# POOL's side steps and the x add of a four-block kernel, each held behind what is written before it on its engine

## The chip, the cores and the metric

The kernel runs on one core of one Trainium2 chip. The metric is device time in microseconds (us) of one execution. Before the change three executions took 3738.57, 3738.6 and 3734.69 us; the median is 3738.57 us.

## What is computed

`x` has shape (4, 1024, 128). Four blocks follow one another, each of the form

```
xn = layernorm(x)
s  = attention-like branch of block i on xn
g  = silu(feed-forward-like branch of block i on xn)
x  = x + s * g
```

- Block 0: windowed attention with rotary positions, 16 heads of 8; the other branch is a channel mix.
- Block 1: causal attention; the other branch is a mixture of 8 experts, of which each token uses 2.
- Block 2: full attention followed by a feed-forward network of its own (`_ffn`: residual sum, layernorm, 128 to 512 to 128, residual sum). The other branch is a switch layer: each token goes to one of 8 experts, at most 80 tokens to each.
- Block 3: a state-space (Mamba) block; the other branch is two layers of local attention with gated feed-forward.

The switch layer of block 2 in the reference, shortened:

```python
probs = softmax(tokens @ gate_w + gate_b)
expert_idx = argmax(probs)
pos = position of the token in its expert's queue
keep = pos < 80
dispatch = tokens placed by (expert, pos)          # scatter
h = gelu(dispatch @ w1 + b1)
expert_out = h @ w2 + b2
out = expert_out gathered by (expert, pos) * gate_prob   # 0 where not kept
```

## The kernel before

The rows are held as 32 tiles of 128 tokens by 128 channels, 8 tiles for each of 4 batches. `xn` and `s` stay in on-chip memory for all batches. `x` itself is parked in device memory between blocks. The program is written as Python lists of small steps. `_interleave` mixes several lists into one written order: the longest list sets the number of turns, and in each turn every list, in the order given, is advanced to the same share of its length.

A planner then decides the order of issue on each engine. It goes by its own estimates of when each instruction's inputs are there and takes what is ready, so an instruction may be issued ahead of ones that are written before it on its engine. `keep_in_program_order` adds an edge from an instruction to the one written just before it on the same engine: issue order only, with no wait for the other to finish. All matmuls and transposes of TensorE already have it (`_mm`, `_tr`, L78 and L82). Nothing on the other engines has it before the change. Each engine works its queue in order, so an instruction that waits also holds what is queued behind it.

Attention of blocks 0 to 2 (`_attention`) goes in 16 units, n = 4b + g for batch b and group g of 4 heads. In unit n the following are interleaved, in this order:

- `ahead`: the row maxima of the next units (PE products into `max_ps`, L78; DVE reduction into `neg`, L344), then the split of `neg` into three bf16 parts on POOL (L163 to L166) and its spreading into rows of q (PE, DVE L368, DMA L371). The split for unit n+1 stands in unit n, near 60% of it.
- `weights`: scores on PE (`sc`), exponentials on ACT (L417), products with the values on PE. In units 4, 8 and 12, the first of a batch, the end of the batch before is put in as well: `finish(b)` writes its part of `s` (L504 or L506).
- for g = 0 to 2, a part of `project(b+1)`: both halves of q and the first half of k for g = 0; the second half of k and the stores for g = 1; the values for g = 2. In block 2 a half of q or k is moved out of PSUM by ACT (L232, L235), multiplied with the rotary tables on POOL (L236 to L238) and after the second half split into three parts, also on POOL (L163 to L166).
- the side steps that a plan assigns to the unit.

The plan of block 2 (`_blocks12`, units 0 to 15) is:

| units | side steps |
|---|---|
| 0 to 2 | update of block 1 for batch 3, and the switch's logits |
| 3 | routing: `rows`, the place of every token |
| 4 to 8 | `sends`: 32 scatters of a tile of `xn` into `sent`, indirect DMAs issued by POOL (L1039); 6, 6, 7, 6 and 7 of them |
| 5 to 7, 9 to 11, 13 to 15 | `_ffn` of batch 0, 1, 2: POOL sum `s += xn` (L789), layernorms (DVE L60, L61, L63, L69 and POOL L65), POOL bias sum (L793), then hidden and output products, DVE sum (L787) |
| 9 to 11 | the experts: load of `sent` (SP, L1051), products, store into `back` (L1077) |
| 12, 13, 15 | `gates(b)` of batch 0, 1, 2: 8 gathers from `back` into `xn`, indirect DMAs issued by POOL (L1083), a pause, the weighing on POOL (L1086), Silu on ACT (L653) |
| 13, 14 | `_end_steps` of batch 0 and 1: the update (below) and a copy on POOL (L1781) |

After unit 15 come `_ffn` of batch 3 beside `_end_steps(2)` and `gates(3)`, and last `_end_steps(3)`. The update (`_update_steps`, used at the end of blocks 0, 1 and 2 for every batch, twelve times in all) fetches x, multiplies `xn = s * xn` on POOL (L151), adds `x += xn` on DVE (L148), stores x (L149, SP queue) and normalizes for the next block.

Full attention has 32 maxima steps per unit, 12 of which are done a unit early; with the split and the spreading that makes 34 steps of `ahead`, and with the end of the batch before 38 steps of `weights` in units 4, 8 and 12. In block 2 POOL has nothing else to do in a unit than the split, the rope where there is a projection, and the side steps. In blocks 0 and 1 it also masks the weights (L387).

Of the kernel before, what the change touches and what calls it, by code (L numbers as in the profile page):

```python
# [25 lines left out]
ALU = mybir.AluOpType  # L26
# [3 lines left out]
P = 128  # L30
B, T, C = 4, 1024, 128
NT = T // P
# [21 lines left out]
def _layernorm_parts(k, src, dst):  # L54

    nc, n = k.nc, src.shape[1]
    st = k.small.tile([P, n, 6], F32, tag="ln_st", name="ln_st")
    mv = k.small.tile([P, n, 2], F32, tag="ln_mv", name="ln_mv")
    for i in range(n):
        nc.vector.bn_stats(out=st[:, i, :], in_=src[:, i, :])  # L60
        nc.vector.bn_aggr(out=mv[:, i, :], in_=st[:, i, :])  # L61
    ve = k.small.tile([P, n], F32, tag="ln_ve", name="ln_ve")
    nc.vector.tensor_scalar_add(ve, mv[:, :, 1], EPS)  # L63
    rs = k.small.tile([P, n], F32, tag="ln_rs", name="ln_rs")
    nc.gpsimd.tensor_tensor(rs, ve, k.neghalf[:, :n], ALU.pow)  # L65

    def apply():
        for i in range(n):
            nc.vector.tensor_scalar(  # L69
                dst[:, i, :], src[:, i, :], mv[:, i, 0:1], rs[:, i : i + 1], ALU.subtract, ALU.mult  # L70
            )

    return apply


def _mm(k, *args, **kw):

    k.tc.keep_in_program_order(k.nc.tensor.matmul(*args, **kw))  # L78
# [3 lines left out]
    k.tc.keep_in_program_order(k.nc.tensor.transpose(*args))  # L82


def _ps1(k, name, shape=(P, 512), dtype=F32):

    return k.ps.tile(list(shape), dtype, tag="s", name=name, bufs=3)


def _ps2(k, name):  # L90

    return k.ps.tile([P, 2, 512], F32, tag="m", name=name, bufs=2)


def _to_fm(k, src, dst, scale=None, bias=None):

    nc, n = k.nc, src.shape[1]
    ps = _ps1(k, "tr_ps", (P, 4, P))
    for i in range(n):
        _tr(k, ps[:, i, :], src[:, i, :], k.ident)  # L100
    flat = ps[:, :n, :].rearrange("p a b -> p (a b)")
    if scale is None:
        nc.scalar.copy(dst, flat)
    else:
        nc.vector.tensor_scalar(dst, flat, scale, bias, ALU.mult, ALU.add)


def _norm_steps(k, src, dst):

    held = {}  # L110

    def part(i):
        a = slice(4 * i, 4 * i + 4)
        return [
            lambda: held.update({i: _layernorm_parts(k, src()[:, a, :], dst[:, a, :])}),
            lambda: held.pop(i)(),
        ]

    (a0, b0), (a1, b1) = part(0), part(1)
    return [a0, a1, b0, b1]  # L120
# [10 lines left out]
def _x_tile(k, of):  # L131
    x = k.xpool.tile([P, NT, C], F32, tag="x", name="x", bufs=2)
    k.nc.sync.dma_start(x, of)
    return x


def _update_steps(k, b, of):

    nc = k.nc
    a = slice(b * NT, b * NT + NT)  # L140
    s, g = k.s[:, a, :], k.xn[:, a, :]
    held = {}

    def fetch():
        held["x"] = _x_tile(k, of)

    def add():
        nc.vector.tensor_tensor(held["x"], held["x"], g, ALU.add)  # L148
        nc.sync.dma_start(k.parked[b], held["x"])  # L149

    steps = [fetch, lambda: nc.gpsimd.tensor_tensor(g, s, g, ALU.mult), None, add]  # L151
    return steps + _norm_steps(k, lambda: held["x"], g)


# [495 lines left out]
def _silu_steps(k, batches):  # L650
    g = k.xn
    return [
        lambda a=slice(b * NT, b * NT + NT): k.nc.scalar.activation(g[:, a, :], g[:, a, :], AF.Silu)  # L653
        for b in batches
    ]
# [85 lines left out]
def _ffn(k, pool, w, b):  # L741


    nc, s, xT = k.nc, k.s, k.xT
    a = slice(b * NT, b * NT + NT)
    held = {}

    def norm(i):
        c = slice(b * NT + 4 * i, b * NT + 4 * i + 4)
        held["x", i] = xn = pool.tile([P, 512], F32, tag="side", name="ln_x", bufs=2).rearrange(  # L750
            "p (n c) -> p n c", c=C
        )
        held["n", i] = _layernorm_parts(k, s[:, c, :], xn)

    def to_fm(i):
        _to_fm(k, held.pop(("x", i)), xT[:, b, 1 + 512 * i : 513 + 512 * i], w["g2"], w["be2"])

    def hidden(n, f2):
        hp = _ps2(k, "hp2")
        held["h", n, f2] = h = pool.tile([P, 2, 512], F32, tag="pt", name="h2", bufs=5)  # L760
        for ff in range(2):
            f = 2 * f2 + ff
            rhs = xT[:, b, 1 + 512 * n : 513 + 512 * n]
            _mm(k, hp[:, ff, :], lhsT=w["f1"][:, f * P : f * P + P], rhs=rhs, start=True, stop=True)
            nc.scalar.activation(h[:, ff, :], hp[:, ff, :], AF.Relu, bias=w["fb1"][:, f : f + 1])

    def output(n, f2):
        h = held.pop(("h", n, f2))
        if f2 == 0:
            held["op", n] = _ps1(k, "op2", (P, 4, P))  # L770
        op = held["op", n]


        for c in range(4):
            for ff in range(2):
                _mm(
                    k,
                    op[:, c, :],
                    lhsT=h[:, ff, c * P : c * P + P],
                    rhs=w["f2"][:, 2 * f2 + ff, :],  # L780
                    start=f2 == 0 and ff == 0 and c == 0,
                    stop=f2 == 1 and ff == 1,
                    skip_group_check=True,
                )
        if f2 == 1:
            to = s[:, b * NT + 4 * n : b * NT + 4 * n + 4, :]
            nc.vector.tensor_tensor(to, to, held.pop(("op", n)), ALU.add)  # L787

    steps = [lambda: nc.gpsimd.tensor_tensor(s[:, a, :], s[:, a, :], k.xn[:, a, :], ALU.add), None]  # L789
    for i in range(2):  # L790
        steps += [lambda i=i: norm(i), None, lambda i=i: held.pop(("n", i))(), lambda i=i: to_fm(i)]
    bias = w["fb2"].unsqueeze(1).to_broadcast([P, NT, P])
    steps.append(lambda: nc.gpsimd.tensor_tensor(s[:, a, :], s[:, a, :], bias, ALU.add))  # L793
    for n in range(2):
        steps += [lambda n=n: hidden(n, 0), lambda n=n: hidden(n, 1)]
        steps += [lambda n=n: output(n, 0), lambda n=n: output(n, 1)]
    return steps
# [79 lines left out]
def _blocks12(k, t, wp, pool_of, gates, last, weights):  # L877
# [58 lines left out]
    with pool_of("a2") as pool:  # L936
        rope = pool.tile([P, 2, T], F32, name="rope")
        nc.sync.dma_start(rope, t["rope"][:, 1])
        begin, rest = _attention(k, pool, "full", xT, wb, s, rope)
        _interleave(moe(pool, B - 1), begin)  # L940
        route, experts, gates = _switch(k, pool, wp, t, lg2)

        plan = {}
        _put(plan, to_block2(B - 1, pool), range(3))
        _put(plan, route, [3])
        for b in range(B - 1):
            _put(plan, _ffn(k, pool, wb, b), _behind(b))
        sends, layers = experts
        _put(plan, sends, range(4, 9))
        _put(plan, layers, range(9, 12))  # L950
        for b in range(B - 1):
            _put(plan, gates(b), [12 + b + b // 2])
            if b < 2:
                _put(plan, _end_steps(k, b), [13 + b])
        rest(plan)
        steps = _ffn(k, pool, wb, B - 1)
        _run(steps[:2])
        _interleave(steps[2:], _end_steps(k, B - 2) + gates(B - 1))
        _run(_end_steps(k, B - 1))


def _switch(k, pool, wp, t, lg):
# [7 lines left out]
    nc, xn = k.nc, k.xn  # L970
# [3 lines left out]
    prob = pool.tile([P, NTILE], F32, name="prob")  # L974
    sent = k.tc.dram_tile([NS + P, C], F32, name="sent")
    back = k.tc.dram_tile([NS + P, C], F32, name="back")
# [12 lines left out]
    held = {}  # L989
# [30 lines left out]
    def place():  # L1020
# [12 lines left out]
        nc.vector.tensor_tensor(base, base, place, ALU.mult)  # L1033
        nc.vector.tensor_scalar(rows, base, own[:, 1:2], None, ALU.add)

    row_of = lambda n: bass.IndirectOffsetOnAxis(ap=rows[:, n : n + 1], axis=0)

    def send(n):
        nc.gpsimd.indirect_dma_start(out=sent, out_offset=row_of(n), in_=xn[:, n, :], in_offset=None)  # L1039

    def fetch(e):
        w1, w2 = (wp.tile([P, 512], F32, tag="ew", name="ew", bufs=3) for _ in range(2))
# [36 lines left out]
    def gates(b):  # L1079
        a = slice(b * NT, b * NT + NT)  # L1080

        def fetch(n):
            nc.gpsimd.indirect_dma_start(out=xn[:, n, :], out_offset=None, in_=back, in_offset=row_of(n))  # L1083

        def weigh():
            nc.gpsimd.tensor_tensor(  # L1086
                xn[:, a, :], xn[:, a, :], prob[:, a].unsqueeze(2).to_broadcast([P, NT, C]), ALU.mult
            )

        return [lambda n=n: fetch(n) for n in range(b * NT, b * NT + NT)] + [None, weigh] + _silu_steps(k, [b])  # L1090

    sends = [lambda n=n: send(n) for n in range(NTILE)]
    experts = [load, None, turn, lambda: fetch(0)]
    for e in range(E8):
# [940 lines left out]
```

## Time and profile before

| what | value |
|---|---|
| median of three executions | 3738.57 us |
| the profiled execution | 3753.32 us |
| its span, first to last instruction | 3751.6 us |
| mean granted PE clock | 0.915 |
| PE busy | 3242.6 us, 86% |
| DVE busy | 2440.5 us, 65% |
| ACT busy | 1985.6 us, 53% |
| POOL busy | 1440.0 us, 38% |
| sends L1039 | 32, first at 1793.8, last at 1892.5 us |
| gathers L1083 | 32, first at 2368.7, last at 2655.7 us |
| sums L789 | 4, first at 1887.4, last at 2643.1 us, 2.34 us each |
| products L151 | 12, 2.35 us each |
| adds L148 | 12, 1.23 us each in the median |

The page gives busy times by engine, the span in slices, the DMA queues and the costliest groups of instructions. A query of the trace gives for a stretch of time the busy time of each engine, the instructions of one engine in order (start, duration, engine, line, operation, output and input, and in brackets how long the engine had been idle and what released it), and who waited for whom. A wait for several things is put down to the one that came last.

### The profile page before, as it was taken

To read this page: it belongs to the slowest core of one execution; us is meant where nothing else is said; L and a number is where in the kernel's file an instruction comes from. 1 tells how busy PE (TensorE), PEld (TensorE's weight loads), DVE (VectorE), ACT (ScalarE), POOL (GpSimd) and SP (SyncE) were. 2 spreads that over 40 slices of the span, in tenths; PEclk is the share of its full clock that TensorE was granted. 3 is DMA by queue.
4 is the path that set the end of the run, shared out by engine and by line. 5 is a ranking of instruction groups with operands and counts; after the bars stand their busy time and mean duration, and the time that the engine had idled before them with its cause. 6 is when DMAs were issued, how large, how long until landed. Compare 5 with 4: busy or idle time off the path is not lost. (4 is left out here: it accounts for less than half of the span.)

```text
span 3751.6 us, 64824 instructions
## 1 busy us (share of the span) xinstructions
PE 3242.6 (86%) x24729; PEld 1738.2 (46%) x24729; DVE 2440.5 (65%) x4924; ACT 1985.6 (53%) x4189; POOL 1440.0 (38%) x1972
## 2 busy tenths in 40 slices
PE   5889999999898895899679998678589999989897
PEld 3545555654343432533223333222256667666665
DVE  6666654457757751788567675572478888877785
ACT  2444453346545552266456576456266666766674
POOL 5564554012313224030330210310476677656663
PEclk8998898999979987999889999789789999999999
DMA  3222212112212102111111021110211001011110
GB/s 95 68 68 48 60 39 85 39 32 48 55 29 65 38 14 59 33 36 26 33 39 26 22 60 36 41 26 1 71 25 21 18 20 27 20 24 23 27 24 22
DMA packets 132806, 144.96 MB, mean 39 GB/s; under 512 B 80264, under 2 KB 107792, under 8 KB 125328
## 3 DMA queue, kind: packets, MB, share of 16 engines
q1 hardware_dynamic: 130448, 136.62, 15.0%
q0 software_dynamic: 2048, 4.20, 0.4%
q8 instruction: 196, 3.21, 0.3%
q14 instruction: 114, 0.93, 0.1%
HBM read 92.72 MB, written 30.08 MB: 33 GB/s over the span
## 5 line engine op out<-in xcount | busy, mean ns | idle before, releaser
L417 ACT ACTIVATE pt<-sc 128x512 f32<-128x512 f32 (+3 forms) x2432 | 1077.0, 512 | 872.3 <-PE sc L78 845.7
L344 DVE TENSOR_REDUCE neg<-max_ps 128x1 f32<-128x1024 f32 (+6 forms) x1088 | 1178.4, 1102 | 503.6 <-PE max_ps L78 490.0
L78 PE MATMUL max_ps<-k,q 72*128 72x512 bf16 (+3 forms) x2304 | 673.0, 362 | 140.2 <-DVE neg L344 93.8
L78 PE MATMUL sc<-q,k 75*128 75x512 bf16 (+3 forms) x2432 | 680.3, 354 | 108.0 <-ACT pt L417 84.5
L78 PE MATMUL o_ps<-pt,va 128*32 128x512 f32 (+3 forms) x4864 | 584.8, 550 | 3.1 <-POOL pt L387 2.8
L387 POOL TENSOR_SCALAR_AFFINE_SELECT pt<-pt 128x256 f32<-128x256 f32 (+2 forms) x768 | 292.4, 398 | 615.3 <-ACT pt L417 612.9
L78 PEld LDWEIGHTS <-k 75*128 75x128 bf16 x2432 | 188.2, 101 | 538.3 <-issue 446.3
L78 PEld LDWEIGHTS <-q 72*128 72x128 bf16 x2304 | 227.8, 101 | 435.9 <-issue 313.7
L163 POOL CAST negp<-neg 128x32 bf16<-128x32 f32 x48 | 10.0, 209 | 806.2 <-DVE neg L344 805.9
L1593 ACT ACTIVATE pr<-lsc,nb,r 128x128 f32<-128x128 f32 x512 | 202.1, 475 | 61.5 <-DVE nb L1585 57.9
L1514 POOL TENSOR_TENSOR qn<-qn,rot 128x512 f32<-128x512 f32 x128 | 165.7, 1300 | 143.5 <-DVE rot L1506 127.8
L1523 POOL TENSOR_TENSOR rn<-ss,neghalf 128x16 f32<-128x16 f32 x64 | 188.7, 2949 | 66.7 <-DVE ss L1521 56.9
L78 PEld LDWEIGHTS <-ident 128*128 128x128 bf16 x1472 | 151.6, 103 | 106.0 <-issue 42.7
L78 PEld LDWEIGHTS o_ps<-pt,va 128*32 128x32 f32 x4864 | 101.2, 111 | 206.7 <-issue 167.7
L691 ACT ACTIVATE h<-hp,eb 128x512 f32<-128x512 f32 x128 | 80.8, 683 | 204.7 <-PE hp L78 197.1
L78 PE MATMUL hp<-xT,ew 128*128 128x512 f32 x256 | 132.8, 644 | 28.7 <-ACT rope_t L235 16.4
L1431 PE MATMUL qk_ps<-wqkv,hT 128*128 128x512 f32 x256 | 136.7, 618 | 24.1 <-DVE hT L1477 10.3
L78 PE MATMUL max_ps<-mask_window,ident 128*128 128x134 bf16 (+2 forms) x960 | 139.1, 228 | 0.0
L78 PEld LDWEIGHTS op<-ew,h 128*128 128x128 f32 x1024 | 125.8, 195 | 20.1 <-issue 17.7
L701 DVE SCALAR_TENSOR_TENSOR xn<-op,gates,xn 128x128 f32<-128x128 f32 x256 | 72.1, 345 | 94.3 <-PE op L78 94.3
L78 PE MATMUL op<-ew,h 128*128 128x128 f32 x1024 | 127.7, 279 | 0.0
L1582 DVE TENSOR_REDUCE top<-lsc 128x4 f32<-128x512 f32 x128 | 82.6, 683 | 43.7 <-PE lsc L1431 43.5
(346 smaller groups left out, 5492.1 us busy)
## 6 DMA issues: line engine op xcount, KB each, us to landing
q<-qx SPq DMA_DIRECT2D x144, 192.0 KB
k<-kx SPq DMA_DIRECT2D x432, 64.0 KB
va<-vb SPq DMA_DIRECT2D x120, 128.0 KB
x<-x SPq DMA_DIRECT2D x20, 512.0 KB
qx<-qp SPq DMA_DIRECT2D x12, 768.0 KB
kx<-kp SPq DMA_DIRECT2D x12, 768.0 KB
ew<-in_e1w_dram SPq DMA_DIRECT2D x64, 128.0 KB
x<-in_x_dram SPq DMA_DIRECT2D x8, 512.0 KB
```

Of the source, the lines that this page charges most:

```text
L78: k.tc.keep_in_program_order(k.nc.tensor.matmul(*args, **kw))
L163: eng.tensor_copy(dst[:, 0], src)
L344: nc.vector.tensor_reduce(neg[:, j0 : j0 + m, qt0], of, AX.X, ALU.max, negate=True)
L387: nc.gpsimd.affine_select(out=pt, in_=pt, pattern=[[0, 2], [step, pt.shape[2]]], compare_op=ALU.is_ge, fill=0.0, base=base, channel_multip ...
L417: nc.scalar.activation(pt[:, j % 2, :width], sc[:, :width], AF.Exp, scale=scale)
L691: nc.scalar.activation(h[:, hh, :], hp[:, hh, :], AF.Gelu, bias=eb1[:, e, hh : hh + 1])
L701: nc.vector.scalar_tensor_tensor(to, op[:, c, :], gates[:, 4 * n + c, e : e + 1], to, ALU.mult, ALU.add)
L1431: pin(nc.tensor.matmul(*args, **kw))
L1514: nc.gpsimd.tensor_tensor(qn[:, i], qn[:, i], rot, ALU.add)
L1523: nc.gpsimd.tensor_tensor(rn, ss.rearrange("p w h -> p (w h)"), k.neghalf[:, : 2 * NH], ALU.pow)
L1582: nc.vector.tensor_reduce(top, t.sc[r], AX.X, ALU.max)
L1593: nc.scalar.activation(t.pr[:, h, :], t.sc[r][:, c, :], AF.Exp, bias=t.nb[r][:, c : c + 1], scale=t.r8[:, h : h + 1])
```

## The change

The POOL sums and products of the update, of `_ffn` and of the weighing, both kinds of indirect DMA, and the update's add on DVE are passed through `keep_in_program_order`. What they compute and where they are written stays as it was. `_update_steps` is shared, so its product and its add are held in blocks 0 and 1 as well. The rotary products, the splits, the layernorms, the copy L1781 and everything on ACT and SP are left to the planner.

```diff
+def _tt(k, engine, *args):
+
+    k.tc.keep_in_program_order(engine.tensor_tensor(*args))
...
     def add():
-        nc.vector.tensor_tensor(held["x"], held["x"], g, ALU.add)
+        _tt(k, nc.vector, held["x"], held["x"], g, ALU.add)
         nc.sync.dma_start(k.parked[b], held["x"])
 
-    steps = [fetch, lambda: nc.gpsimd.tensor_tensor(g, s, g, ALU.mult), None, add]
+    steps = [fetch, lambda: _tt(k, nc.gpsimd, g, s, g, ALU.mult), None, add]
...
-    steps = [lambda: nc.gpsimd.tensor_tensor(s[:, a, :], s[:, a, :], k.xn[:, a, :], ALU.add), None]
+    steps = [lambda: _tt(k, nc.gpsimd, s[:, a, :], s[:, a, :], k.xn[:, a, :], ALU.add), None]
...
-    steps.append(lambda: nc.gpsimd.tensor_tensor(s[:, a, :], s[:, a, :], bias, ALU.add))
+    steps.append(lambda: _tt(k, nc.gpsimd, s[:, a, :], s[:, a, :], bias, ALU.add))
...
+    pin = k.tc.keep_in_program_order
     row_of = lambda n: bass.IndirectOffsetOnAxis(ap=rows[:, n : n + 1], axis=0)
 
     def send(n):
-        nc.gpsimd.indirect_dma_start(out=sent, out_offset=row_of(n), in_=xn[:, n, :], in_offset=None)
+        pin(nc.gpsimd.indirect_dma_start(out=sent, out_offset=row_of(n), in_=xn[:, n, :], in_offset=None))
...
         def fetch(n):
-            nc.gpsimd.indirect_dma_start(out=xn[:, n, :], out_offset=None, in_=back, in_offset=row_of(n))
+            pin(nc.gpsimd.indirect_dma_start(out=xn[:, n, :], out_offset=None, in_=back, in_offset=row_of(n)))
 
         def weigh():
-            nc.gpsimd.tensor_tensor(
-                xn[:, a, :], xn[:, a, :], prob[:, a].unsqueeze(2).to_broadcast([P, NT, C]), ALU.mult
-            )
+            _tt(k, nc.gpsimd, xn[:, a, :], xn[:, a, :], prob[:, a].unsqueeze(2).to_broadcast([P, NT, C]), ALU.mult)
```

## The prediction

> **What bounds the kernel now.** I first read the busy shares: PE (TensorE) is busy 86% of the span, DVE 65%, ACT 53%, POOL 38%. PE is the bound, so time is won only where PE stands still. Block 2 runs from about 1440 to 2690 us; its table of 20 us stretches has two places where PE nearly stops (columns: stretch, length, then busy us and count of PE, PEld, DVE, ACT, POOL, PE clock, DMA).
>
> ```profile
> 1820.00:1840.00 20.00, 19.19 (x112) 8.10 (x110) 16.06 (x16) 11.72 (x22) 6.70 (x7) 1.00 0.12 34
> 1840.00:1860.00 20.00, 2.01 (x14) 0.60 (x7) 0.00 (x0) 2.24 (x5) 10.49 (x10) 0.61 0.07 23
> 1860.00:1880.00 20.00, 0.00 (x0) 0.00 (x0) 0.00 (x0) 0.00 (x0) 10.63 (x11) 0.50 0.07 23
> 1880.00:1900.00 20.00, 7.51 (x30) 1.62 (x30) 7.42 (x27) 3.73 (x8) 14.38 (x14) 0.61 0.25 83
> ...
> 2380.00:2400.00 20.00, 0.58 (x1) 0.11 (x1) 3.48 (x2) 6.40 (x8) 15.08 (x11) 0.50 0.25 70
> ...
> 2440.00:2460.00 20.00, 3.75 (x12) 0.54 (x12) 13.67 (x55) 5.69 (x7) 11.66 (x13) 0.54 0.09 28
> ```
>
> In hole A (1842 to 1892) only POOL works. Next the waits in 1835 to 1900, engine by engine (total us, times, longest):
>
> ```profile
> PE max_ps L78 <- DVE neg L344: 49.7, 1, 49.7
> DVE ln_st L60 <- POOL s L789: 51.2, 1, 51.2
> POOL sent L1039 <- DMA sent<-xn,rows: 23.1, 15, 1.6
> ```
>
> So PE waits for row maxima, DVE cannot take them because a layernorm of `_ffn` (L60) stands ahead of them in its queue, and that waits for the sum `s += xn` (L789) on POOL. POOL's timeline says why the sum is late:
>
> ```profile
> 1853.86 0.96 POOL L1039 DMA_INDIRECT sent<-xn,rows  x1 [1.53 <-DMA sent<-xn,rows]
> 1854.84 1.27 POOL L236 TENSOR_TENSOR qd<-qd,rope 128x512 f32<-128x512 f32 x1
> ...
> 1887.45 2.34 POOL L789 TENSOR_TENSOR s<-s,xn 128x1024 f32<-128x1024 f32 x1
> ```
>
> Thirty of the 32 sends run ahead of L789, each 2.49 us after the last. They are written over units 4 to 8 but were issued as soon as `rows` existed. Holes B and C (2372 to 2403, 2438 to 2457), waits in 2335 to 2470:
>
> ```profile
> PE sc L78 <- ACT pt L417: 35.1, 6, 25.4
> PE max_ps L78 <- DVE neg L344: 12.4, 2, 10.1
> ACT L653 <- DMA xn<-back,rows: 17.9, 2, 13.4
> DVE x L148 <- POOL xn L151: 24.3, 2, 21.9
> ```
>
> ```profile
> 2391.68 2.36 POOL L151 TENSOR_TENSOR xn<-s,xn 128x1024 f32<-128x1024 f32 x1
> ...
> 2438.26 0.94 POOL L1083 DMA_INDIRECT xn<-back,rows  x1 [0.31 <-issue]
> 2440.90 1.90 POOL L1086 TENSOR_TENSOR xn<-xn,prob 128x1024 f32<-128x1024 f32 x1 [1.70 <-DMA xn<-back,rows]
> 2442.74 0.21 POOL L163 CAST negp<-neg 128x32 bf16<-128x32 f32 x1
> ```
>
> ACT waits in a Silu, DVE in an `x` add, both for gathers (L1083) of batches 0 and 1 that went together early in unit 12; then batch 2's gathers, written in unit 15, go ahead of the split for unit 13.
>
> [...] 2.2 us to landing, 2.49 us from send to send, with the rope products behind. [...] Two max_ps matmuls take 1.01 us after hole A and 0.60 before it; after B it stays slow for 19 us[...]. [...]
>
> **The change part by part.** Nothing is added or removed: 88 POOL instructions (32 sends, 32 gathers, 12 products L151, 4 sums L789, 4 L793, 4 weighings L1086) and 12 DVE adds L148 get an order edge to the instruction written before them on their engine.
>
> (1) Sends. Six stay in unit 4: one behind the rope of q's first half, the others spread. The unit runs from split to split, 1789.51 to 1894.54, 105.0 us; unit 8, with the same projection steps, 2068.91 to 2134.16, 65.3. Gain by that twin 39.8. By the hole: 49.7 idle plus 3.5 for slow clock (8.6 us after it, 1891.7 to 1896.3 and 1902 to 1906, at 1.01 for 0.60), less 5.6 because DVE waits that long for L789 before unit 9 and may now do so in unit 5: 47.6. I take **43**, between the two. A send that waits 1.5 us for the one before holds the rope and the splits queued behind it, and through them ACT's projections and the neg rows. At 6 or 7 sends in a unit of 50 to 65 us they stand some 8 us apart and POOL is idle more than half of the time (6.1 busy of 20 us in unit 9), so I cost it at nothing; were all of it on the path, it would be 32 x 1.5 = 48.
>
> (2) Gathers, weighings, L151, L148. Steps count out as follows: unit 12 has 38 turns (0 to 37; 32 steps of weights, 2 closing, 4 finishing); the split for unit 13, step 20 of 34, falls in turn 22; of the 11 steps of gates(0), gathers 0 to 6 come before it, gather 7 in turn 24, the weighing in 31, the Silu in 34. So gathers 0 to 6 do not move (they wait for `back` at 2338 to 2368 as now), but gather 7 is behind the split, and with it the weighing, the Silu and later the product and the add. Batch 1 goes to unit 13, batch 2 to 15. Idle gone: 25.4 + 2.3 + 7.8 + 10.1 = 45.6. Slow clock: 18.8 us after B and 5.7 after C at 1.06 for 0.60, 10.6 lost. Sum 56. Given back: three Silus now stand among exponentials: 1.28 + 1.06 + 1.28 = 3.6 us each if the weighing is there in time, 7.8 (PE's wait at C) if not; I take the middle, 5.7 x 3 = 17. DVE now does two of the updates beside the maxima: add 1.2, norms 4.8 (8 pairs of L60 and L61 at 0.28, two fours of L69 at 1.1, two L63 at 0.17), so 6.0 each. Where there are maxima DVE is busy 15.5 of 20 us, which leaves some 14 us in a unit of 60; unit 13 asks for 6.0 and the FFN's norms, 4.8. That fits on average, but the adds stand in DVE's queue with maxima behind them, and PE waits for those: 5 back. Net **34**. Ends: 56 less 3 x 7.8 less all DVE work of the updates and one FFN, 16.8, is 16; 56 less 3 x 3.6 is 45. The store of x behind each add (L149, SP queue) moves a unit later, past that unit's q and k loads; x is read back only in the next block. Zero.
>
> (3) L789 and L793. In units 5 and 9 L789 moves behind the second half of k's rope and split (1929 to 1939.6 now), in unit 13 behind the weighing of batch 0, which is done by then. Queued behind it on POOL: sends and ln_rs; on DVE the layernorm waits. Zero, if DVE's order follows; otherwise it is the slower rival below.
>
> (4) Tail. Gathers 24 to 31 move behind L793, so the second ln_rs of the last FFN no longer stands behind four of them (4.8 us; PE waits 8.4 for ln_x there); L151 of batch 2 comes 2.4 later and is ahead of it. The gathers, 8 x 1.25 us, then have from about 2665 to 2686, when L151 of batch 3 is released by DVE's last sum: 10 + 2.5 landing + 1.9 weighing + 2.3 Silu with its table ends near 2682, so they stay covered, by 4 us. Take **3**, ends -4 and 6.
>
> (5) Blocks 0 and 1: seven L151 and L148 move to their written place. DVE waits 22.0 us for L151 there, six times; PE has other work queued. At best -10, at worst as much more behind mask selects. Zero.
>
> (6) SP. `load` (L1051) waited 6.7 us for the last send with loads queued behind; it meets that in unit 8 or 9. Zero; +7 if the rows of neg are behind it.
>
> Sum: 43 + 34 + 3 = 80. The profiled execution took 3753.3 us (span 3751.6, 1.7 around it); less 80 it is 3673.3. The median, 3738.57, is 0.4% shorter; scaled, 3738.57 x (1 - 80/3753.3) = 3659.
>
> **Rivals.** R1, B and C come back in another form: Silu and add are not pinned to PE's progress and stall again. For: gathers 0 to 6 do not move; against: gather 7 does. Gain 43 + 3 = 46: 3693. R2, more than counted: the twin's own 5.6 us and half of (5)'s 22 go, little is given back: 112, 3627. R3, **slower**: DVE's layernorm of units 5 and 9 keeps its early place while L789 goes behind the k split: 1939.6 - 1887.5 = 52 us in unit 5, 2180.7 - 2127.1 = 53 in unit 9 (both as now). PE stops with DVE, as in hole A. -80 + 105 = +25: 3763. It decides from 40 us per wait. Against it: an instruction's place in its queue is planned after its input's; for it: the 51.2 us above show how wrong planned times can be. R4: the edges change little, since POOL's predecessor may be long done: 3739.
>
> **How the numbers follow.** Likeliest 0.70 (its own range 3640 to 3680), R1 0.14, R2 0.08, R3 0.05, R4 0.03. Within 0.2% (7 us) counts as no change, about what a measurement can tell. Faster 0.92, same 0.03, slower 0.05. The range takes in R1 and R2 with their bounds: 3622 to 3698.
>
> **What would show it.** Right: sends spread over units 4 to 8, PE busy 17 or more in every stretch from 1500 until the tail, ln_st's wait for L789 under 10 us, gather 7 behind a cast of L163. Wrong: PE waiting 20 us or more on Silu or on L148's engine (R1), or ln_st waiting about 50 us twice (R3).

## The result and the profile after

The changed kernel takes 3695.59 us in the median (3685.96 to 3716.14, four runs) beside 3738.59 us for the kernel before on the same chip (four runs): a ratio of 0.9887, 95% interval 0.9838 to 0.9935. The forecast was 3659 us. The direction holds and the time lies inside the range, near its upper end, but outside the likeliest case's own range (3640 to 3680). It lies where R1 ended (3693), which is in part luck, as the account below shows. The profiled execution took 3699.6 us, its span 3697.9 us: 53.7 us less than before, where the sum of the prediction was 80.

Several helpers moved, so L151, L148, L789, L793 and L1086 all read L87 now; L1039 is L1045, L1083 is L1089, L163 is L168, L344 is L349, L417 is L422, L653 is L658, L1781 is L1785.

**Hole A is gone.** The table of 20 us stretches of the kernel after, the same four stretches:

```profile
1820.00:1840.00 20.00, 18.84 (x104) 6.10 (x103) 14.25 (x15) 12.57 (x24) 13.02 (x13) 1.00 0.13 47
1840.00:1860.00 20.00, 18.67 (x107) 5.94 (x99) 12.46 (x13) 13.45 (x27) 5.76 (x5) 1.00 0.03 8
1860.00:1880.00 20.00, 17.05 (x87) 5.72 (x83) 13.08 (x17) 11.22 (x22) 13.47 (x10) 0.98 0.42 103
1880.00:1900.00 20.00, 19.64 (x89) 4.87 (x87) 15.35 (x30) 11.50 (x22) 5.57 (x9) 0.77 0.03 11
```

PE (first pair of columns after the length) is busy 17 us or more in each. POOL's timeline says why:

```profile
1809.63 1.24 POOL L1045 DMA_INDIRECT sent<-xn,rows  x1 [0.19 <-DVE rec L465]
...
1874.90 2.35 POOL L87 TENSOR_TENSOR s<-s,xn 128x1024 f32<-128x1024 f32 x1
...
2017.12 0.96 POOL L1045 DMA_INDIRECT sent<-xn,rows  x1 [1.53 <-DMA sent<-xn,rows]
```

Sends still go out at 2017 (the last at 2089.4), and the sum stands at 1874.9 instead of behind thirty sends.

**Holes B and C have left their places, and new ones stand in units 13 and 14.** The same table there:

```profile
2340.00:2360.00 20.00, 11.01 (x59) 2.88 (x59) 8.43 (x17) 12.44 (x21) 9.39 (x11) 0.84 0.03 8
2360.00:2380.00 20.00, 13.97 (x67) 4.30 (x67) 19.15 (x46) 7.20 (x14) 10.33 (x9) 0.73 0.22 72
...
2420.00:2440.00 20.00, 4.41 (x14) 0.92 (x15) 11.56 (x32) 5.64 (x8) 12.28 (x9) 0.55 0.17 59
2440.00:2460.00 20.00, 16.18 (x58) 4.58 (x56) 8.79 (x8) 11.34 (x18) 6.87 (x7) 0.67 0.07 20
```

In 2420 to 2440 PE is busy 4.4 of 20 us. The waits in 2320 to 2460 and then the three engines' timelines tell how it comes about:

```profile
PE sc L78 <- DVE at L466: 15.9, 1, 15.9
PE sc L78 <- ACT pt L422: 11.4, 8, 5.6
PE max_ps L78 <- DVE neg L349: 8.8, 2, 8.4
DVE x L87 <- POOL xn L87: 9.1, 1, 9.1
DVE ln_st L60 <- POOL s L87: 8.7, 1, 8.7
```

```profile
2419.91 1.89 POOL L87 TENSOR_TENSOR xn<-xn,prob 128x1024 f32<-128x1024 f32 x1 [1.83 <-DMA xn<-back,rows]
2422.97 2.34 POOL L87 TENSOR_TENSOR xn<-s,xn 128x1024 f32<-128x1024 f32 x1 [1.17 <-ACT xn L658]
...
2436.68 1.06 POOL L1089 DMA_INDIRECT xn<-back,rows  x1 [0.18 <-issue]
...
2509.49 0.21 POOL L168 CAST negp<-neg 128x32 bf16<-128x32 f32 x1 [59.44 <-DVE neg L349]
```

```profile
2415.59 0.68 DVE L453 COPY os<-o_ps 128x512 f32<-128x512 f32 x1
2425.34 1.22 DVE L87 TENSOR_TENSOR x<-x,xn 128x1024 f32<-128x1024 f32 x1 [9.07 <-POOL xn L87]
...
2435.26 0.28 DVE L466 TENSOR_TENSOR at<-ot,rec 128x128 f32<-128x128 f32 x1
```

```profile
2419.08 0.60 PE L78 MATMUL max_ps<-k,q 72*128 72x512 bf16 x2
2435.59 1.03 PE L78 MATMUL sc<-q,k 75*128 75x512 bf16 x2 [15.91 <-DVE at L466]
```

In unit 13 PE stands twice, at its start:

```profile
2356.67 0.59 PE L78 MATMUL sc<-q,k 75*128 75x512 bf16 x1 [5.61 <-ACT pt L422]
2365.61 1.01 PE L78 MATMUL max_ps<-k,q 72*128 72x512 bf16 x2 [8.36 <-DVE neg L349]
```

```profile
2353.58 2.34 POOL L87 TENSOR_TENSOR s<-s,xn 128x1024 f32<-128x1024 f32 x1
2355.96 0.49 DVE L60 BATCH_NORM_STATS2 ln_st<-s 128x6 f32<-128x128 f32 x2 [8.70 <-POOL s L87]
```

The first wait is for exponentials behind the Silu of batch 0. The second is for a maximum that stands in DVE's queue behind a layernorm of `_ffn` and the x add of batch 0. The layernorm waits 8.7 us for the sum of batch 2, and the sum stands on POOL behind the weighing of batch 0, which waits for gather 7.

In unit 14 the longest wait is at L466. The update of batch 1 is written in this unit. Its weighing starts at 2419.9, soon after the split at 2415.74 that ends unit 13, as its edge demands. But the x add stands in DVE's queue right after `os` and waits 9.07 us for the product; then follow the norms of the update; only then come the reciprocal and product (L465, L466) for which PE waits. And the gather at 2436.68 is number 16, the first of batch 2: it is written in unit 15, behind the split of 2509.49, and went 73 us ahead of it.

**The tail** is 5.6 us longer. ACT's timeline there, and the PE group that follows:

```profile
2606.72 0.69 ACT L770 ACTIVATE h<-hp,w 128x512 f32<-128x512 f32 x1 [2.17 <-PE hp L78]
2613.93 1.28 ACT L658 ACT_TABLE_LOAD   x1 [6.52 <-DMA xn<-back,rows]
2615.93 1.06 ACT L658 ACTIVATE xn<-xn 128x1024 f32<-128x1024 f32 x1 [0.72 <-POOL xn L87]
2616.89 0.67 ACT L770 ACTIVATE h<-hp,w 128x512 f32<-128x512 f32 x1
```

```profile
2617.61 3.78 PE L78 MATMUL hp<-xT,w 128*128 128x512 f32 x4 [5.05 <-ACT h L770]
```

The Silu of batch 3 stands in ACT's queue between the hidden layer's two halves and waits 6.5 us for gathers that now go out only behind L793.

**The table by stage.** A stage runs from the first cast of one split to that of the next; the 16 splits of block 2 are read from POOL's timeline. Unit 15 ends where the last 16 `wo_ps` products begin, the tail where the first `sh_ps` of block 3 begins. Times are of the profiled executions, in us.

| kernel | first split | u0–3 | u4–8 | u9–11 | u12 | u13 | u14 | u15 | tail | first split to sh_ps |
|---|---|---|---|---|---|---|---|---|---|---|
| before | 1562.3 | 227.2 | 344.6 | 203.0 | 105.5 | 64.2 | 65.0 | 68.3 | 46.5 | 1124.5 |
| after | 1552.5 | 228.1 | 295.9 | 206.9 | 63.9 | 68.4 | 93.8 | 68.3 | 52.1 | 1077.3 |
| sends only | 1556.6 | 227.3 | 301.6 | 205.3 | 102.6 | 63.9 | 65.0 | 68.3 | 44.9 | 1078.8 |
| all but sends | 1546.1 | 225.5 | 328.9 | 200.5 | 62.3 | 70.7 | 91.7 | 68.3 | 50.0 | 1098.0 |
| updates in 0, 1 only | 1550.0 | 224.5 | 343.9 | 202.9 | 105.5 | 64.2 | 65.0 | 68.3 | 44.9 | 1119.3 |
| copy held | 1534.8 | 228.1 | 295.9 | 206.9 | 62.3 | 70.5 | 85.4 | 81.7 | 49.8 | 1080.7 |
| norms and copy held | 1550.1 | 239.7 | 288.2 | 195.9 | 62.4 | 61.1 | 73.4 | 81.4 | 51.5 | 1053.6 |
| end steps first | 1537.3 | 228.0 | 296.0 | 205.4 | 64.6 | 67.0 | 79.1 | 73.3 | 49.6 | 1063.1 |
| tail free | 1554.8 | 228.1 | 296.0 | 203.0 | 62.4 | 70.2 | 93.6 | 68.3 | 44.4 | 1065.9 |
| all three | 1560.8 | 237.9 | 294.5 | 201.6 | 62.3 | 60.9 | 80.6 | 81.4 | 46.7 | 1065.9 |
| own norms, tail free | 1534.4 | 228.1 | 288.2 | 196.0 | 64.6 | 60.4 | 73.2 | 81.5 | 46.7 | 1038.6 |

The table needs two warnings. Up to the first split the kernels after, "copy held" and "end steps first" issue the same instructions in the same order, and that split comes at 1552.5, 1534.8 and 1537.3. So 18 us there is no effect of an edit. The stretch from that split to `sh_ps` is the finer measure: it fell by 47.1 us from before to after.

But inside block 2, too, a unit can differ with no change of order, where PE was granted another clock. In unit 10 the kernels after and "tail free" issue the same instructions in the same order, and PE waits equally (1.5 us at the longest):

| unit 10 | us | PE busy, us | PE clock |
|---|---|---|---|
| before | 63.4 | 58.4 | 0.97 |
| tail free | 65.5 | 60.9 | 0.94 |
| after | 69.8 | 65.3 | 0.87 |

"Norms and copy held" and "all three" have the same order up to unit 13, and differ by 12.0 us in units 4 to 11. A few us in one unit tell of an order only where PE's waits differ as well.

### The profile page after: what moved, and what is told of

It is laid out like the page before. It is cut to its first block, busy times and chain, and to the rows that moved or that the text cites. A ratio compares the mean times of both kernels' runs of the same rounds, so it can differ in the third digit from the quotient of the medians.

```text
span 3697.9 us, 64830 instructions
## 1 busy us (share of the span) xinstructions
PE 3251.8 (88%) x24727; PEld 1738.3 (47%) x24729; DVE 2437.4 (66%) x4924; ACT 1991.1 (54%) x4191; POOL 1443.5 (39%) x1972
## 5 line engine op out<-in xcount | busy, mean ns | idle before, releaser
L422 ACT ACTIVATE pt<-sc 128x512 f32<-128x512 f32 (+3 forms) x2432 | 1079.1, 511 | 853.6 <-PE sc L78 817.6
L349 DVE TENSOR_REDUCE neg<-max_ps 128x1 f32<-128x1024 f32 (+6 forms) x1088 | 1178.6, 1102 | 525.4 <-PE max_ps L78 507.4
L78 PE MATMUL sc<-q,k 75*128 75x512 bf16 (+3 forms) x2432 | 684.8, 356 | 112.8 <-ACT pt L422 60.9
L78 PE MATMUL o_ps<-pt,va 128*32 128x512 f32 (+3 forms) x4864 | 591.5, 553 | 14.7 <-POOL pt L392 9.8
L168 POOL CAST negp<-neg 128x32 bf16<-128x32 f32 x48 | 10.2, 212 | 722.7 <-DVE neg L349 722.5
L65 POOL TENSOR_TENSOR ln_rs<-ln_ve,neghalf 128x4 f32<-128x4 f32 x72 | 73.7, 1025 | 128.9 <-DVE ln_ve L63 124.6
```

What stands on the lines that cost most here:

```text
L349: nc.vector.tensor_reduce(neg[:, j0 : j0 + m, qt0], of, AX.X, ALU.max, negate=True)
L422: nc.scalar.activation(pt[:, j % 2, :width], sc[:, :width], AF.Exp, scale=scale)
```

## The experiments

Theory: an edge ties an instruction only to the one written just before it on its engine. Where that one is itself held, or is a split that waits for row maxima, the instruction stays in place; where it is a norm or a copy left to the planner, both float together and run ahead. Rivals are named in each expectation. Medians are set against the kernel before on the same chip.

**1. Sends only** (`e1_sends_only`, from the kernel before)

```diff
-        nc.gpsimd.indirect_dma_start(out=sent, ...)
+        k.tc.keep_in_program_order(nc.gpsimd.indirect_dma_start(out=sent, ...))
```

> The kernel before with the order edge on the 32 sends alone. Theory 1 (each edge holds only to the instruction written just before; the sends carry the whole gain): unit 4, split to split, falls from 105.0 to about 57 us, unit 12 stays near 105 with its two holes, the tail to the first shift product stays 46.5; total about 3738 - 48 = 3690, so equal to the changed kernel within its noise. Theory 2 (the gain needs the sum of the FFN behind the k split as well): DVE waits some 10 to 50 us for the sum before unit 5, total 3700 to 3735.

Measured: 3695.88 us (six runs), ratio 0.986 (0.9803 to 0.9917). Units 4 to 8 take 43.0 us less than before, block 2 as a whole 45.7. Holes B and C stay (unit 12: 102.6). In block 2 the edges on the sends alone give nearly what all edges give together (47.1).

**2. All but the sends** (`e2_all_but_sends`, from the kernel after)

```diff
-        pin(nc.gpsimd.indirect_dma_start(out=sent, ...))
+        nc.gpsimd.indirect_dma_start(out=sent, ...)
```

> The changed kernel with the sends left to the planner. Theory 1: hole A comes back (unit 4 about 105 us), units 12 to 15 as in the changed kernel (294 us from the split of unit 12 to the last wo product, against 303 before), tail 52 us; total 3738 - 9 + 6 = about 3735. Theory 2 (gathers, weighings and updates carry part of the gain): 3700 to 3725.

Measured: 3719.31 us (18 runs), ratio 0.9937 (0.9913 to 0.996): the other edges gain more than theory 1 allowed, 26.5 us in block 2, and the time lies in the range of theory 2. Of the 26.5 us 15.7 lie in units 4 to 8, though the sends are as bunched as before (mostly 2.49 us from send to send in both). The waits in 1780 to 1900:

```profile
ACT kd L237 <- POOL qp L171: 36.6, 1, 36.6
PE max_ps L78 <- ACT rope_t L240: 36.3, 2, 35.8
```

The hole is 36 us where it was 49.7, and it has another name: DVE no longer waits for the sum, but ACT now waits for POOL's rope and split of q, which stand among the sends, and PE for ACT. The bunch is the cause, and whichever engine needs POOL first reports it. The two halves don't add: 45.7 and 26.5 make 72.2, together they are 47.1. Of the 25 us between, 10 lie in units 4 to 8, where both shorten hole A. The rest lies in the other stages, 2 to 5 us in each, and stays open; in units 0 to 3 and 9 to 11 profiles of one order differ by as much.

**3. Updates of blocks 0 and 1 only** (`e7_updates_01`, from the kernel before: L151 and L148 get the edges, until block 2's attention begins)

```diff
+    if not getattr(k, "free", False):
+        k.tc.keep_in_program_order(ins)
...
+        k.free = True
         begin, rest = _attention(k, pool, "full", xT, wb, s, rope)
```

> The kernel before with the edges on product and add of the updates in blocks 0 and 1 only; block 2 is left to the planner. Theory A (these edges gain there): the first split of block 2 comes at 1537 to 1553 us, as in the four profiles that have them, against 1557 and 1562 without, total about 12 us under before. Theory B (blocks 0 and 1 differ from run to run by as much, edges or not): no difference clear of the interval, and waits of DVE for the product near 22 us or less with PE as busy as before.

Measured: 3742.8 us (20 runs), ratio 1.0001 (0.9977 to 1.0025). Nothing, within 0.25%. The first split comes at 1550.0, where theory A wanted it, but that sign decides nothing: "all three" has these edges too and comes at 1560.8.

**4. The copy held too** (`e3_copy_held`, from the kernel after, as are all that follow)

```diff
-    ... [lambda: nc.gpsimd.tensor_copy(k.s[:, a, :], k.xn[:, a, :])]
+    ... [lambda: k.tc.keep_in_program_order(nc.gpsimd.tensor_copy(k.s[:, a, :], k.xn[:, a, :]))]
```

> The changed kernel with one more edge, on the copy of s (L1785) that ends an update. Theory 1: in unit 14 the copy is the last thing written on POOL ahead of gathers 16 to 23, and it stands behind the split for unit 15; held, it keeps them there: they go after the last cast of a split (2509 us in the changed kernel) instead of at 2437, with batch 2's Silu in unit 15; unit 14 gets shorter by 4 to 8 us and unit 15 longer by as much, the 15.9 us hole stays, since no edge of DVE is touched. Theory 2 (gathers go when the data are there, whatever the edge): they stay near 2437.

Measured: one run, 3681.72 us, no interval. POOL's timeline:

```profile
2484.05 0.21 POOL L168 CAST negp<-neg 128x32 bf16<-128x32 f32 x1 [66.87 <-DVE neg L349]
...
2485.12 1.04 POOL L1785 COPY s<-xn 128x1024 f32<-128x1024 f32 x1
2486.32 1.06 POOL L1089 DMA_INDIRECT xn<-back,rows  x1 [0.16 <-issue]
```

Gather 16 is written right after L1785 on POOL. With that copy held it stands behind the split. That shows why it escaped. Where the time goes: unit 14 is 8.4 us shorter and unit 15 13.4 longer, so it is no gain; both are more than expected. The Silu of batch 2 now stands among exponentials of unit 15, where ACT waits 7.2 us for the gathers and pays two table loads (1.28 us each), and PE waits up to 11.8 us for a hidden activation behind it.

**5. Norms and copy held** (`e4_norms_held`: the same edge on bn_stats, bn_aggr, the sum with EPS, the power and the final scaling of every layernorm, and on L1785, within the units of block 2)

```diff
+        _hold(k, nc.vector.bn_stats(out=st[:, i, :], in_=src[:, i, :]))
+        _hold(k, nc.vector.bn_aggr(out=mv[:, i, :], in_=st[:, i, :]))
...
+        k.hold = True
         rest(plan)
+        k.hold = False
```

> The changed kernel with edges also on every instruction of the layernorms (DVE and POOL) and on the copy of s in block 2's units, not in its tail. Theory 1 (the add and the gathers of batch 2 escape their unit because what is written just before them, a layernorm or the copy, is itself free): the add stays in its unit, the burst of norms in front of the maxima is gone, gathers 16 to 23 go behind the split for unit 15; unit 14 falls from 93.8 to 65 to 72 us, total about 25 us under the changed kernel, 3670. Theory 2 (the holes of units 12 to 14 are the Silu's wait for gathers and weighing, whatever DVE does): PE still waits 10 to 20 us in units 12 to 14 on exponentials, total within 8 us of the changed kernel.

Measured: 3669.43 us (six runs), ratio 0.9799 (0.9744 to 0.9853). Unit 14 falls from 93.8 to 73.4, just above the 65 to 72 expected, and unit 13 from 68.4 to 61.1. The 15.9 us wait at L466 is gone (no wait of PE in unit 14 is over 2.1 us), and the 8.4 us wait for a maximum in unit 13 is 0.4. Units 4 to 11 fall by 18.8, of which 3.9 are unit 10 and its clock. Against that, unit 15 is 13 us longer, as in experiment 4, and units 0 to 3 lose 11.6, since the norms of block 1's last update stand in them and are held as well. Net 23.7 us in block 2.

**6. The end steps written ahead of the feed-forward's** (`e5_end_first`: order of writing in a turn alone, no further edge)

```diff
+        for b in range(2):
+            _put(plan, _end_steps(k, b), [13 + b])
         for b in range(B - 1):
             _put(plan, _ffn(k, pool, wb, b), _behind(b))
```

> The changed kernel with one edit: in units 13 and 14 the end steps are written ahead of the FFN's steps of the same turn, so that what stands just before the x add on DVE is a maximum or a normalization of the attention and not a layernorm of the FFN. Theory 1: the two adds are issued in the middle of their units, DVE waits under 3 us for the product in unit 14 (9.1 in the changed kernel) and the 15.9 us hole shrinks; the norms behind stay free, so part of the burst remains; total 8 to 20 us under the changed kernel. Theory 2: no difference beyond 5 us.

Measured: 3666.41 us (six runs), ratio 0.9793 (0.9746 to 0.9841). Unit 14 is 79.1: of its 28.8 extra us 14.7 are gone, 5.0 of which come back in unit 15. The x add is now not written right behind a free norm of `_ffn`; it is issued in the middle of unit 14, and DVE no longer waits for the product. Experiments 5 and 6 reach the same add in two ways and its wait is gone in both, so its predecessor is what decided that wait. It is not the whole hole. PE still waits here at the head of unit 14:

```profile
2412.40 1.03 PE L78 MATMUL sc<-q,k 75*128 75x512 bf16 x2 [10.87 <-DVE at L466]
```

Ahead of L466 on DVE stand the free norms of batch 0's update and of `_ffn`, which wait 1.7 and 3.2 us for POOL. Only with the norms held as well (experiment 5) does this wait vanish. The gathers of batch 2 also go later, at 2464.3, so that their Silu leaves unit 14 for unit 15.

**7. Tail without edges** (`e6_tail_free`)

```diff
         rest(plan)
+        k.free = True
         steps = _ffn(k, pool, wb, B - 1)
```

> The changed kernel without the edges in the tail (the last FFN, the updates of batches 2 and 3, gates of batch 3). Theory: the tail, last wo product to first shift product, goes from 52.1 back to 45 to 47 us, because the Silu of batch 3 stood in ACT's queue ahead of the last hidden layer and waited for gathers held behind the bias sum. Rival (the tail is longer because batch 2's update now falls into it, edges or not): 50 us or more.

Measured: one run, 3684.18 us. The tail is 44.4 us, 7.7 less, and the rival is out. The waits of ACT in 2560 to 2640 there:

```profile
ACT L664 <- DMA xn<-back,rows: 21.8, 1, 21.8
ACT h L776 <- PE hp L78: 14.0, 8, 3.8
```

The Silu waits even longer, but it now stands ahead of the whole hidden layer (L776 is L770 here), at 2594, where PE has nothing for ACT to do.

**8. Experiments 5 to 7 together** (`e8_all_held`; the three edits above)

> The changed kernel with three edits together: layernorms and copy held in block 2's units, end steps written ahead of the FFN's, no edges in the tail. Theory 1: gains add up in part: from the first split of block 2 to the first shift product about 1040 us (1077 in the changed kernel, 1054 with the layernorms held, of which 12 fell in units 1 and 2), total about 3655.

Measured: 3664.65 us (seven runs), ratio 0.9798 (0.9757 to 0.9839). The stretch of block 2 missed its expectation: 1065.9. But the profile is that of the slowest of the seven executions (3690.87 us), and what is longer in it than with norms and copy alone is PE's clock. Unit 6 takes 60.3 us at a clock of 0.89 (54.0 at 1.00 in experiment 5), unit 10 71.0 at 0.86 (66.0 at 0.93), unit 14 80.6 at 0.83 (73.4 at 0.93): 18.6 us together, with PE's longest wait equal in each (0.7, 1.5 and 2.1 us). So this run does not show that the edits cost each other time. Writing the end steps first brought nothing beyond holding the norms: unit 13 is 60.9 beside 61.1.

**9. Block 2's own norms and copy held, tail free** (`e10_ffn_norms_tail`: experiment 5 without the norms of block 1's last update, plus experiment 7)

```diff
-        _put(plan, to_block2(B - 1, pool), range(3))
+        _put(plan, [loose(step) for step in to_block2(B - 1, pool)], range(3))
```

`loose` sets `k.hold` to False while its step is written.

> The norms of block 2's own steps (the feed-forward networks and the end updates) and the copy are held behind what is written before them; the norms of block 1's last update, in units 0 to 2, and the steps after unit 15 are left to the planner, as before the change. Escape theory: units 0 to 3 return to about 228 us (239.7 with all norms held), unit 4 stays near 57, units 5 to 8 near 231, units 13 and 14 together near 135 (162 after the change), the tail 44 to 47. From the first split of block 2 to the first sh_ps product that makes about 1035 us (1077.3 after the change, 1053.6 with all norms held), and a time of 3645 to 3660. Rival (the hold that lengthens one place gives another place its time, as the combination of all holds showed, so nothing more is to be had): 1055 to 1070 and a time of 3664 to 3680.

Measured: 3650.59 us (six runs), ratio 0.9778 (0.975 to 0.9806): faster than both kernels, and its interval lies below that of the change (0.9838 to 0.9935). Every stage named came within 2 us of the expectation: units 0 to 3 are back at 228.1, units 13 and 14 together take 133.6, the tail 46.7. The stretch of 1038.6 is 38.7 us less than after the change, of which 6.5 are unit 10 and its clock (0.97 for 0.87). Most of units 13 and 14 (2311.28 to 2444.83) in the table of stretches:

```profile
2360.00:2380.00 20.00, 17.61 (x98) 5.25 (x97) 19.03 (x46) 13.39 (x26) 6.93 (x9) 1.00 0.10 37
2380.00:2400.00 20.00, 16.29 (x83) 4.93 (x83) 14.48 (x18) 12.67 (x21) 4.98 (x4) 0.91 0.10 32
2400.00:2420.00 20.00, 17.31 (x98) 5.24 (x96) 16.38 (x27) 12.92 (x26) 3.37 (x2) 1.00 0.07 27
2420.00:2440.00 20.00, 19.17 (x110) 6.03 (x109) 16.88 (x39) 14.32 (x28) 4.34 (x3) 1.00 0.00 1
```

From 2320 to 2440 no stretch has PE below 16 us; the work of the updates (DVE, third pair) lies beside the maxima, as the prediction had pictured it for the change itself. Two waits of PE behind a Silu are left: 5.5 us at the start of unit 13, and 11.6 us for a hidden activation in unit 15, which is 13.2 us longer than after the change.

## Why the prediction was right or wrong

**(1) Sends: right.** 43 was taken. Unit 4 fell by 47.6 us, from 105.0 to 57.4; by the hole's working it was to be 47.6, by the twin 39.8. The sends alone gave 45.7 us in block 2. That the measured figure meets the hole's to a tenth is luck. That waiting sends would cost nothing held within a few us: with sends alone, units 5 to 8 take 240.9 us beside 239.6 before. They do not stand some 8 us apart, though: in units 6 and 7 six or seven of them go 2.5 us apart, right behind the split (1899.4 to 1914.5 in unit 6). An edge sets an order and no pace. POOL then stands idle until the next split, 36.7 us in unit 6.

**(2) Gathers, weighing, product, add: the old holes went, the give-back failed, +34 expected and +8.8 measured** (units 12 to 15). Gather 7 did land behind the split:

```profile
2347.32 0.21 POOL L168 CAST negp<-neg 128x32 bf16<-128x32 f32 x1 [23.74 <-DVE neg L349]
...
2348.61 0.98 POOL L1089 DMA_INDIRECT xn<-back,rows  x1
```

and unit 12, which held hole B and the first 4.7 us of hole C, fell by 41.7 us. The rest of C, 13.2 us of idle PE, lay in unit 13 and is replaced there by the 14.0 us shown above, so that unit 13 is 4.2 us longer instead of shorter. What failed is the give-back: 56 less 8.8 is 47, where 17 + 5 = 22 was allowed. Of the 45.6 us of idle PE that were to go, 33.7 stand in units 13 and 14 in a new form:

- The Silus, for which 17 was allowed, show 5.6 us on PE in unit 13 (batch 0) and 3.8 in unit 14 (batch 2; ACT takes table load, Silu and table load, 1.28, 1.06 and 1.28 us, from 2448.1 to 2452.4, and PE's `sc` waits). That of batch 1 is hidden in the wait at L466.
- DVE's queue, for which 5 was allowed, shows 8.4 us in unit 13 and 15.9 in unit 14, together 24.3. This is the term that was mis-sized.
- The slow clock after these new waits was not counted: pairs of `max_ps` products take up to 1.06 us for 0.60 over 5.3 us in unit 13 and over 19.7 us in unit 14, which loses about 2 us and 9. In unit 14 PE is busy 71.1 us at a clock of 0.82 with what took 61.9 at 1.00 before. With it some 45 of the 47 us are found.

Three statements of the prediction were wrong. "Behind the split, and with it the weighing, the Silu and later the product and the add" followed the edges only for POOL. On DVE the add of batch 1 is written right after the scaling of a layernorm of `_ffn` (L69), which the change leaves to the planner, so the add came early and waited (9.07 us), and the update's norms with it. "Batch 2 to 15" was wrong as well: gather 16 hung on a free copy. And the sum of unit 13 was to stand behind a weighing "which is done by then"; see (3). The number of adds and norms that I counted for DVE was right; that this "fits on average" hid that they come in one burst, with waits for POOL in it.

**(3) Sums: right in units 5 and 9, wrong in unit 13.** In units 4 to 11 the layernorm's longest wait for a sum is 4.1 us. R3's 52 us twice did not come: DVE's norms moved with their input, as the argument against it said. But in unit 13 gather 7 lands behind the split, the weighing of batch 0 comes behind the gather and the sum behind the weighing. The layernorm waits 8.7 us there, and PE 8.4 behind it, so a wait under 10 us, the sign named for being right, was not yet harmless. With the norms held (experiment 5) PE's wait is 0.4 us.

**(4) Tail: wrong sign, +3 expected and −5.6 measured,** 1.6 us beyond the end of −4. What +3 was taken for did come: PE's waits for `ln_x` in the tail fall from 18.3 to 14.7 us. The gathers' times were right as well (2602.5 to 2612.4, spaced 1.25, the Silu done at 2617.0), and they are ahead of L151, which starts at 2629.9. What was missed is ACT's own queue, in which the Silu's wait of 6.5 us held up what stood behind it, as L60's of 51.2 us did on DVE in hole A: the Silu was compared with DVE's last sum and not with the hidden layer's activations queued behind it, for which PE now waits 7.6 us in all, 3.3 before. The rest of the 5.6 us goes with PE's clock, 0.64 in this tail and 0.71 before. Five profiles with the edges in the tail have 49.6 to 52.1 us, six without them 44.4 to 46.7, so the loss is there, of some 3 to 8 us.

**(5) Blocks 0 and 1: right at zero.** DVE's waits for L151 did go; the groups of the add in all blocks, before and after:

```profile
L148 DVE TENSOR_TENSOR x<-x,xn 128x1024 f32<-128x1024 f32 x12 | 18.7, 1559 | 51.5 <-POOL xn L151 51.5
```

```profile
L87 DVE TENSOR_TENSOR x<-x,xn 128x1024 f32<-128x1024 f32 x12 | 14.6, 1217 | 11.6 <-POOL xn L87 11.6
```

Of 51.5 us of waiting 11.6 are left, all of it in block 2 (9.1 in unit 14, 2.5 in the tail), and the time of blocks 0 and 1 is the same (ratio 1.0001): this fits that PE had other work queued, as said. The half of it that R2 hoped for is not there.

**(6) SP: right at zero.** The load of `sent` now waits 19.7 us for the last send, where it was 6.7; PE shows no wait for it, and unit 9 is 2.0 us shorter than before.

The change of the times in block 2: units 0 to 3 +0.9 us, 4 to 8 −48.7, 9 to 11 +3.9, 12 to 15 −8.8, tail +5.6, together −47.1. The +3.9 of units 9 to 11 is unit 10, 6.4 us longer at a lower clock, and no effect of the order is shown in it. The rest of the profiled difference (−9.8 ahead of the first split, +3.2 in block 3) is of the size by which runs of the same order differ.

Of the signs named ahead, spread sends, the layernorm's wait under 10 us and gather 7 behind a cast came true; "PE busy 17 or more in every stretch" did not. R1 was right in its reason: Silu and add, not pinned to PE's progress, stall again, in units 13 and 14, though no single wait reaches the 20 us it asked for. That its sum of 46 us meets the measured fall of 43 in the medians is in part luck: against its 43 for the sends and 3 for the tail stand 48.7 in units 4 to 8, 8.8 in units 12 to 15, and losses of 5.6 in the tail and of 3.9 in unit 10's clock. It deserved more than 0.14.

## What to carry to other kernels

An order edge to the instruction written just before is as firm as that instruction: before counting on it, name the predecessor on the same engine for every held instruction, and ask what holds that one. When a long queue in front of a shared engine is spread, the gain can be read from a twin stage (39.8 here, 47.6 measured); when consumers on several engines have to follow, cost each engine's queue apart, the activation behind the Silu as well as the reduction behind the add. Judge by stages, and for each stage by its waits and its granted clock beside its length: here the start of block 2 moved by up to 18 us, and one unit by up to 6, between profiles of one order.

## What was not expected of the hardware

- After the 15.9 us hole in unit 14 pairs of `max_ps` products take 1.06 us until 2445.5 and 0.60 from 2446.5 on: some 10 us slow, at a granted clock of 0.51 from 2435.6 to 2446.0. Some 3 us at 1.00 later, a gap of 3.82 us is followed by a second slow stretch of 9.2 us, from 2453.6 to 2462.8, at 0.50. In unit 10 one of 9.9 us (2159.5 to 2169.4, at 0.51) follows a gap of only 1.45 us. So the slow stretches after these two short gaps are about as long as the one after the long hole; what sets their length was not shown.
- Executions of one kernel on one chip differ by as much as the edits bring, and they follow the mean clock that PE was granted: 27 of the kernel before run from 3716.19 us at a clock of 0.927 to 3767.42 at 0.911. Stages are finer but not free of it. Units 0 to 3 take 228.0 to 228.1 in five kernels whose order is the same there, but 227.2 and 224.5 in two others; unit 10 moves by 4.3 and unit 6 by 6.4 between two kernels of one order.
